# A graph network's last layer: eight outputs of each edge are summed over their 16 terms on VectorE before TensorE sums over the edges

## The chip, the cores and the metric

One core of a Trainium2 chip runs the whole program. The metric is device time in microseconds. A core has TensorE (PE, matrix products, with PEld for its weight loads), VectorE (DVE), ScalarE (ACT), GpSimd (POOL, which here issues indirect gathers) and SyncE (SP, which issues plain transfers). Each engine works through its own list in order, and they wait for one another through semaphores. TensorE writes into PSUM banks (`bank`); all else lies in SBUF, here in one large tile `f_arena`.

## The reference

Four graph layers run one after another over 8192 nodes of 32 values and 262144 edges sorted by destination. Each layer computes a message per edge, sums the messages at their destination, adds the result to the node and normalizes. The change is in the last layer. There an edge has its own weights, made from its 32 features by a small network:

```python
h = jax.nn.relu(edge_feat @ W1 + b1)
w = (h @ W2 + b2).reshape(e, 4, MUL, MUL)          # MUL = 8: 256 weights per edge
m0 = ALPHA * (einsum('ei,eio->eo', s_e * sh0, w_000)
              + C110 * einsum('eim,em,eio->eo', v_e, sh1, w_110))
m1 = ALPHA * (einsum('ei,em,eio->eom', s_e, sh1, w_011)
              + einsum('eim,eio->eom', v_e * sh0, w_101))
out0 = segment_sum(m0, dst); out1 = segment_sum(m1, dst)
```

Here s is the first 8 values of the source node, v the other 24 (8 vectors of 3), and sh the four values of the edge. So m0 has eight outputs per edge, each a sum of 8 + 8 = 16 products, and m1 has 24.

## The kernel before

Layers 0 to 2 run first and are untouched. Layer 3 goes over the edges in 512 quads. A quad `q` is four columns of 128 edges; eight quads make a batch `s` of 32 columns. Two quads, a pair, make one aggregation group `g` of 1024 edges.

For each quad the program does this:

- **Gather.** GpSimd fetches the source nodes' rows, one indirect transfer per column, 12 quads ahead (`fetch_rows`, `AHEAD = 12`, transfer at L380). The four gathers of quad q + 12 wait until quad q's weights are made (`quad[q]["w"]`).
- **Hidden layer.** Every second quad, `hidden` makes `h` for two quads: two matmuls (L836) and two ScalarE activations (L844).
- **Weights.** Four matmuls (L860) put the 4 x 256 weights into one of two PSUM buffers (`w_bank`). They wait for VectorE to be done with the quad before last.
- **Products on VectorE.** L897 multiplies weights with s for the w_011 part, and the result `pr` is reduced to 8 values one turn later (L889) and multiplied with sh into 24 columns (L884, two turns later). L900 makes the 128 products of m0 (8 outputs of 16 terms), and the three L904 make the 192 products of the w_101 part. L502 makes the one-hot matrix of destinations. The mark after L502 is `quad[q]["v"]`.
- **Sum over edges.** Four matmuls (L869) take the one-hot matrices as stationary operand and the products `p` as moving operand and add 1024 edges into a bank of 344 columns: 128 products of m0, 192 of the w_101 part and 24 finished. They stand three quads later in TensorE's list and wait for the mark `v` of the quad after next.
- **Evacuation.** After each second quad VectorE reduces the bank: 128 to 8 (L926), 192 to 24 (L927), and adds the 24 finished columns (L929) into the window `win`. Later `windows` and `normalize` put windows together into nodes.

Every eight quads `factors` (L778 to L789) prepares the next batch's `a0` and `vm` on VectorE.

The order on each engine is written out by hand in one loop `for q in range(NQ + 4)`. In a turn q, TensorE gets hidden(q + 2) on even turns, then the weights of q, then the sum over the edges of q - 3. VectorE gets, after `factors` where due, L884 of q - 2, L889 of q - 1, then waits for the weights of q and does L897, L900, L904 three times and L502, and on turns with q - 3 odd the evacuation. `p` has five buffers (`NP`), `pr` and `red` two.

Of the kernel before, what the change touches and what calls it, by code (L numbers as in the profile page):

```python
# [16 lines left out]
OP = mybir.AluOpType  # L17
AX = mybir.AxisListType
# [87 lines left out]
def in_order(ctx: ExitStack, tc, x, a, w0, w1, b1, w2, si, keep):  # L106
# [34 lines left out]
    with tc.tile_critical():  # L141
        raw_layers(tc, x, a, w0, w1, b1, w2, si, m, bad)
# [3 lines left out]
def raw_layers(tc, x, a, w0, w1, b1, w2, si, m, bad):  # L146
    nc = tc.nc
    PE, V, A, G, S = (Flow(tc, e, n) for e, n in ((nc.tensor, "pe"), (nc.vector, "dve"), (nc.scalar, "act"),
                                                  (nc.gpsimd, "pool"), (nc.sync, "sp")))
    bank, arena = m["bank"], m["arena"]  # L150
# [41 lines left out]
    cut = Carve()  # L192
# [10 lines left out]
    win = cut(GG, D)  # L203
    end0 = cut.at

    cut = Carve(8192)
    rg = cut(64, MS, 3)
    rgi = rg.rearrange("p a b c -> p (a b c)").bitcast(I32).rearrange("p (a b c) -> p a b c", b=MS, c=3)
    cut = Carve(8192)
    nxt = cut(TT, dt=I32)  # L210
    base = cut(GG, GT, dt=I32)
    cut = Carve()
# [177 lines left out]
    for j in range(NB // 4):  # L390
        for c in range(4):
# [4 lines left out]
            for h in range(2):  # L396
# [3 lines left out]
                for q in (2 * h, 2 * h + 1):  # L400
                    ins = PE.e.matmul(bank[:, 2 * b + q % 2, :], xT[q * D:(q + 1) * D, j, :],
                                      w0_s[q * D:(q + 1) * D, c * 512:(c + 1) * 512], start=True, stop=True)
# [3 lines left out]
                o, yp = ys[:, u, 2 * h:2 * h + 2, :], bank[:, 2 * b:2 * b + 2, :]  # L406
# [16 lines left out]
    def gathers(table, ix, s, t0=0, n=WT):  # L423

        if t0 == 0:
            state["n"] += 1
        k = (state["n"] - 1) % 4
        for t in range(t0, t0 + n):
            ld = g_ld[k][t // TP]
            if t % TP == 0:  # L430
                G.after(taken[k][t // TP])
                if len(under_way) >= LAG:
                    G.after(under_way[-LAG])
            indirect(xg[:, k, t, :], table[:, :], ix[:, s * WT + t:s * WT + t + 1]).then_inc(ld.sem, 16)
            ld.n += 16
            if t % TP == TP - 1:
                under_way.append(ld.mark())
        return k, under_way[-(WT // TP):]
# [58 lines left out]
    def ready(c):  # L497

        return min(GG, 4 * (LC * (c + 1) - 1) + 5)
# [93 lines left out]
    for g in range(GG):  # L593
        s, h, bk, c = g * GT // WT, g % NO, (g // per) % 2, g % per
        if g == FIRST // 2:
            V.after(slots(), x_in)
        if g * GT % WT == 0:
            k, landed = gathers(ytab, row, s)
# [5 lines left out]
        for t in range(GT):  # L604
            ins = PE.e.matmul(bank[:, bk, c * D:(c + 1) * D], oh[:, h, t, :], xg[:, k, g * GT % WT + t, :],  # L605
                              start=(t == 0), stop=(t == GT - 1))
# [17 lines left out]
    cut = Carve()  # L624
# [47 lines left out]
    for n, (l, c) in enumerate(seq):  # L672
# [8 lines left out]
        for s in range(64):  # L681
            if l == 1:
                q = s % 4
                ins = PE.e.matmul(bank[q * D:(q + 1) * D, b, 0:256].rearrange("p (u h j) -> p u h j", h=2, j=4),  # L684
                                  x_b[:, s, :], mv[:, s], start=(s < 4), stop=(s >= 60), tile_position=(0, q * D))
            else:
                ins = PE.e.matmul(bank[0:96, b, 0:512].rearrange("p (u h j) -> p u h j", h=2, j=4),  # L687
                                  x3[:, s, :], mv[:, s], start=(s == 0), stop=(s == 63))
# [13 lines left out]
    cut = Carve()  # L702
    xg = cut(4, WT, D)
    win = cut(GG, D)
# [13 lines left out]
    vs = cut(WT, 8, 3)  # L718
    a1 = cut(WT, 8)
    vm = cut(2, WT, 3, 8)  # L720
    MW = 344
    NP, NO = 5, 5
    p = cut(NP, 4, MW)
    pr = cut(2, 4, 64)
    red = cut(2, 4, 8)
    oh = cut(NO, 4, P)
    r1 = cut(24)
# [36 lines left out]
    def fetch_rows(q):  # L764

        if q < NQ:
            G.after(quad.get(q - AHEAD, {}).get("w"))
            rows[q // 8] = gathers(xtab, src, q // 8, q % 8 * 4, 4)
# [55 lines left out]
    def w_bank():  # L824
        k = nxt[0] % 2
        nxt[0] += 1
        return k, bank[:, 3 + 2 * k:5 + 2 * k, :].rearrange("p b (h c) -> p (b h) c", c=256)
# [24 lines left out]
    for q in range(NQ + 4):  # L852

        if q % 2 == 0 and q + 2 < NQ:
            hidden(q + 2)
        if q < NQ:
            k, wp = w_bank()
            PE.after(quad[q]["h"], w_free[k])
            for t in range(4):
                ins = PE.e.matmul(wp[:, t, :], hs[0:65, q % 4, t * P:(t + 1) * P], w2_s[0:65], start=True, stop=True)  # L860
            quad[q]["w"] = PE.mark(ins)
            quad[q]["k"] = k, wp
            fetch_rows(q + AHEAD)
        c = q - 3
        if 0 <= c < NQ:
            g = c // 2
            PE.after(quad[c + 2]["v"], agg_free[g % 2] if c % 2 == 0 else None)
            for t in range(4):
                ins = PE.e.matmul(bank[:, g % 2, 0:MW], oh[:, c % NO, t, :], p[:, c % NP, t, :],  # L869
                                  start=(c % 2 == 0 and t == 0), stop=(c % 2 == 1 and t == 3))  # L870
            quad[c]["a"] = PE.mark(ins)

        prev = (V.sem, V.n)
        if q % 8 == 6 and q // 8 + 1 < NS:
            s = q // 8 + 1
            factors(s)
        V.after(prev)
        if q < NQ:
            V.after(batch[q // 8]["f"])
        V.after(quad.get(q - NP, {}).get("a"))  # L880
        ins = None
        if 0 <= q - 2 < NQ:
            c = q - 2
            ins = V.e.tensor_tensor(p[:, c % NP, :, 320:344].rearrange("p t (o m) -> p t o m", m=3),  # L884
                                    red[:, c % 2, :, :, None].to_broadcast([P, 4, 8, 3]),
                                    sh[:, (c // 8) % 3, (c % 8) * 4:(c % 8) * 4 + 4, None, 1:4].to_broadcast([P, 4, 8, 3]),
                                    op=OP.mult)
        if 0 <= q - 1 < NQ:
            ins = V.e.tensor_reduce(red[:, (q - 1) % 2], pr[:, (q - 1) % 2].rearrange("p t (o i) -> p t o i", i=8),  # L889
                                    AX.X, OP.add)  # L890
        if q < NQ:
            k, wp = quad[q]["k"]
            s, u = q // 8, (q // 8) % 2
            qs = slice((q % 8) * 4, (q % 8) * 4 + 4)
            pq = p[:, q % NP]
            V.after(quad[q]["w"])
            V.e.tensor_tensor(pr[:, q % 2].rearrange("p t (o i) -> p t o i", i=8),  # L897
                              wp[:, :, 128:192].rearrange("p t (o i) -> p t o i", i=8),
                              xg[:, batch[s]["xg"], qs, None, 0:8].to_broadcast([P, 4, 8, 8]), op=OP.mult)
            V.e.tensor_tensor(pq[:, :, 0:128].rearrange("p t (o k) -> p t o k", k=16),  # L900
                              wp[:, :, 0:128].rearrange("p t (o k) -> p t o k", k=16),
                              a0[:, u, qs, None, :].to_broadcast([P, 4, 8, 16]), op=OP.mult)
            for mm in range(3):
                V.e.tensor_tensor(pq[:, :, 128 + 64 * mm:192 + 64 * mm].rearrange("p t (o i) -> p t o i", i=8),  # L904
                                  wp[:, :, 192:256].rearrange("p t (o i) -> p t o i", i=8),
                                  vm[:, u, qs, mm, None, :].to_broadcast([P, 4, 8, 8]), op=OP.mult)
            ins = one_hot(oh[:, q % NO], 4 * q, 4)
        if ins is not None:
            d = V.mark(ins)
            if q < NQ + 2:  # L910
                quad.setdefault(q, {})["v"] = d
            if q < NQ:
                w_free[k] = d
                if 4 * (q + 1) % TP == 0:
                    taken[batch[s]["xg"]][4 * (q % 8) // TP] = d
            if 0 <= q - 2 < NQ and (q - 2) % 8 == 7:
                s = (q - 2) // 8
                sh_free[s % 3] = d
                if s + 3 < NS:
                    fetch(s + 3)  # L920

        c = q - 3
        if 0 <= c < NQ and c % 2 == 1:
            g = c // 2
            V.after(quad[c]["a"])
            V.e.tensor_reduce(win[:, g, 0:8], bank[:, g % 2, 0:128].rearrange("p (o k) -> p o k", k=16), AX.X, OP.add)  # L926
            rm = V.mark(V.e.tensor_reduce(r1, bank[:, g % 2, 128:320].rearrange("p (mo i) -> p mo i", i=8), AX.X, OP.add))  # L927
            V.after(rm)
            gm = V.mark(V.e.tensor_tensor(win[:, g, 8:].rearrange("p (o m) -> p o m", m=3),  # L929
                                          bank[:, g % 2, 320:344].rearrange("p (o m) -> p o m", m=3),  # L930
                                          r1.rearrange("p (m o) -> p o m", o=8), op=OP.add))
            agg_free[g % 2] = gm
            while done < NB // LC and ready(done) <= g + 1:
                k, wp = w_bank()
                acc = bank[:, 3 + 2 * k, 0:LC * D]
                w_free[k] = normalize(3, done, acc, windows(done, acc, (w_free[k], gm)), z, x_a)
                done += 1
# [471 lines left out]
```

## Time and profile before

| | us |
|---|---|
| median of 3 runs | 7803.98 (7796.38 to 7807.71) |
| the profiled execution | 7682.45 |
| its span, first to last instruction | 7680.7 |
| busy in the span: TensorE | 5868.9 (76%) |
| VectorE | 3758.9 (49%) |
| ScalarE | 1653.0 (22%) |
| GpSimd | 4001.1 (52%) |
| layer 3, 4720 to 7560: TensorE, VectorE, GpSimd busy | 2540.9, 1956.5, 1873.0 of 2840 |

The profile is of one execution, and this one is shorter than the median of the timed runs by 121.5 us. A row of a group view gives the line, engine and operation, what it writes and reads, the shape, how many, the busy time and the mean of one in ns, and then the idle time of the engine just before these instructions with what ended most of it. An f32 matmul leaves two records, so four matmuls show as eight. The ends of matmuls are modelled, and a few records can be missing. In a timeline row stand the start, the duration, the engine, the line, the operation, and in brackets how long the engine had been idle before it and what is taken to have released it.

### The profile page before, as it was taken

The page shows a single profiled execution, that of the slowest core. Times are in us where ns is not written, and L with a number is a line of the kernel's source. Part 1 is how long each engine was busy: PE and PEld are TensorE (multiplying, and loading weights), DVE is VectorE, ACT ScalarE, POOL GpSimd, SP SyncE. Part 2 cuts the span into 40 slices and gives each one's busy share as a digit, 9 for nine tenths or more (in the row PEclk, how much of TensorE's full clock was granted, in tenths as well). Part 3 has the DMA queues.
Part 4 walks back from the last instruction along what each step waited for, and adds up shares of the span by engine and source line. Part 5 has one row for each costly group of instructions (what it writes and reads, how often), then busy time and mean ns, then how long its engine had stood idle before and what let it go on. Part 6 is the DMA issues. An engine that isn't in the chain of part 4 may idle for free.

```text
span 7680.7 us, 88486 instructions
## 1 busy us (share of the span) xinstructions
PE 5868.9 (76%) x36084; PEld 4261.6 (55%) x36084; DVE 3758.9 (49%) x6691; ACT 1653.0 (22%) x2828; POOL 4001.1 (52%) x4174
## 2 busy tenths in 40 slices
PE   5327777787877778786444776989898889888898
PEld 2116767776767667676222344555555555555555
DVE  3304444444444454544000004666666766676666
ACT  3123333333333333333000001111111111111111
POOL 3456656565656656561000006666666666666663
PEclk7556777777777777777777887999999899999999
DMA  8405655555555555567999981111111111111111
GB/s 285 144 10 125 144 141 143 142 145 140 143 142 145 148 134 151 136 149 217 432 432 429 403 336 26 24 24 24 24 24 27 24 24 24 24 24 24 24 24 19
DMA packets 290736, 999.46 MB, mean 130 GB/s; under 512 B 99022, under 2 KB 175887, under 8 KB 250639
## 3 DMA queue, kind: packets, MB, share of 16 engines
q1 hardware_dynamic: 155742, 916.89, 33.0%
q0 software_dynamic: 134144, 73.67, 9.4%
q8 instruction: 286, 4.69, 0.3%
q10 hardware_dynamic: 432, 3.15, 0.1%
q14 instruction: 132, 1.07, 0.1%
HBM read 521.39 MB, written 471.99 MB: 129 GB/s over the span
## 4 chain that ended last, share of the span: by engine, by line
PE 51%; DVE 15%; another core or an unknown queue 15%; DMA 10%; issue 6%; ACT 3%; SPq 0%; DVEq 0%; ACTq 0%
PE bank L869 16%; PE bank L568 15%; PE bank L860 9%; DMA f_arena<-famat 6%; PE bank L605 3%; PE bank L836 3%; DMA f_arena<-fcmat 3%; DVE f_arena L904 3%; DVE f_arena L502 2%; DVE f_arena L556 2%; PE bank L684 2%; PE bank L687 2%; DVE f_arena L900 2%; ACT f_arena L573 1%
## 5 line engine op out<-in xcount | busy, mean ns | idle before, releaser
L380 POOL DMA_INDIRECT f_arena<-fxtab,f_src x2048 | 1971.8, 963 | 2135.8 <-DVE f_arena L740 1111.0
L380 POOL DMA_INDIRECT f_arena<-fytab,f_row x2048 | 1962.0, 958 | 1338.6 <-issue 552.8
L568 PE MATMUL bank<-f_arena 64*128 64x128 f32 x16384 | 1846.0, 376 | 580.1 <-issue 416.2
L568 PEld LDWEIGHTS bank<-f_arena 64*128 64x128 f32 x16384 | 1619.5, 275 | 792.3 <-issue 572.6
L869 PE MATMUL bank<-f_arena 128*128 128x344 f32 x4096 | 1486.7, 511 | 288.6 <-DVE f_arena L502 284.2
L869 PEld LDWEIGHTS bank<-f_arena 128*128 128x128 f32 x4096 | 860.2, 214 | 764.2 <-DVE f_arena L502 348.7
L572 ACT ACTIVATE f_arena<-bank 128x512 bf16<-128x512 f32 x1024 | 612.3, 598 | 1886.7 <-remote 1163.8
L860 PE MATMUL bank<-f_arena 65*128 65x256 f32 x4096 | 1005.2, 388 | 0.0
L554 DVE TENSOR_TENSOR f_arena<-bank,f_arena 128x1024 f32<-128x1024 f32 x256 | 313.3, 1224 | 1363.4 <-remote 1281.6
L860 PEld LDWEIGHTS bank<-f_arena 65*128 65x128 f32 x4096 | 762.5, 191 | 357.3 <-issue 223.0
L844 ACT ACTIVATE f_arena<-bank,f_arena 64x512 f32<-64x512 f32 x512 | 351.1, 686 | 2530.8 <-PE bank L836 909.5
L502 DVE TENSOR_TENSOR f_arena<-bank,f_rel 128x512 f32<-128x512 f32 (+1 forms) x768 | 659.1, 859 | 246.1 <-ACT f_arena L534 233.6
L605 PE MATMUL bank<-f_arena 128*128 128x32 f32 x4096 | 545.3, 283 | 125.4 <-DMA f_arena<-fytab,f_row 69.0
L573 ACT ACTIVATE f_arena<-bank 128x512 f32<-128x512 f32 x1024 | 607.7, 593 | 0.0
L605 PEld LDWEIGHTS bank<-f_arena 128*128 128x128 f32 x4096 | 509.8, 199 | 155.2 <-issue 107.3
L556 DVE TENSOR_TENSOR f_arena<-bank,f_arena 128x2048 f32<-128x2048 f32 x256 | 586.6, 2291 | 8.8
L904 DVE TENSOR_TENSOR f_arena<-bank,f_arena 128x256 f32<-128x256 f32 x1536 | 551.3, 415 | 0.0
L684 PE MATMUL bank<-f_arena,f_x_b 128*32 128x256 f32 x4096 | 293.9, 458 | 335.5 <-DMA f_arena<-famat 335.5
L897 DVE TENSOR_TENSOR f_arena<-bank,f_arena 128x256 f32<-128x256 f32 x512 | 215.9, 422 | 660.8 <-PE bank L860 288.0
L684 PEld LDWEIGHTS bank<-f_arena,f_x_b 128*32 128x32 f32 x4096 | 145.5, 131 | 472.6 <-DMA f_arena<-famat 309.8
L900 DVE TENSOR_TENSOR f_arena<-bank,f_arena 128x512 f32<-128x512 f32 x512 | 348.8, 681 | 0.0
L687 PE MATMUL bank<-f_arena 128*96 128x512 bf16 x1024 | 248.7, 405 | 80.1 <-DMA f_arena<-fcmat 80.1
(127 smaller groups left out, 2628.1 us busy)
## 6 DMA issues: line engine op xcount, KB each, us to landing
famat<-f_arena SPq DMA_DIRECT2D x256, 1024.0 KB
fcmat<-f_arena SPq DMA_DIRECT2D x256, 512.0 KB
fytab<-f_arena SPq DMA_DIRECT2D x64, 1024.0 KB
f_arena<-fytab,f_row POOLq DMA_INDIRECT x2048
f_arena<-fxtab,f_src POOLq DMA_INDIRECT x2048
f_arena<-laid_ea SPq DMA_DIRECT2D x64, 512.0 KB
f_arena<-laid_ea SPq DMA_DIRECT2D x64, 64.0 KB
f_arena<-laid_xT ACTq DMA_DIRECT2D x1, 1024.0 KB, 8.0
```

The source lines that it names most:

```text
L380: return G.e.indirect_dma_start(out=dest, out_offset=None, in_=table, in_offset=bass.IndirectOffsetOnAxis(ap=ix, axis=0))
L502: return V.e.tensor_tensor(o, iota[:, None, :].to_broadcast([P, n, P]), rel[:, t:t + n, None].to_broadcast([P, n, P]), op=OP.is_equal)
L556: V.e.tensor_tensor(oh_l[:, b], iota[:, None, :].to_broadcast([P, 16, P]), meta_l[:, pp, k0:k0 + 16, None].to_broadcast([P, 16, P]), op=OP ...
L568: ins = PE.e.matmul(bank[:, bk + h, :].rearrange("p (c s j) -> p c s j", s=64, j=4)[:, :, :, j], oh_l[hs_, b, 4 * q + j, :], oh_k[hs_, b, ...
L572: A.e.activation(st_c[:, b, q], bank[:, bk:bk + 2, 0:256], AF.Copy)
L573: bank_free[units[0] % 2] = am = A.mark(A.e.activation(st_a[:, b, q], bank[:, bk:bk + 2, 256:512], AF.Copy))
L605: ins = PE.e.matmul(bank[:, bk, c * D:(c + 1) * D], oh[:, h, t, :], xg[:, k, g * GT % WT + t, :], start=(t == 0), stop=(t == GT - 1))
L684: ins = PE.e.matmul(bank[q * D:(q + 1) * D, b, 0:256].rearrange("p (u h j) -> p u h j", h=2, j=4), x_b[:, s, :], mv[:, s], start=(s < 4), ...
L860: ins = PE.e.matmul(wp[:, t, :], hs[0:65, q % 4, t * P:(t + 1) * P], w2_s[0:65], start=True, stop=True)
L869: ins = PE.e.matmul(bank[:, g % 2, 0:MW], oh[:, c % NO, t, :], p[:, c % NP, t, :], start=(c % 2 == 0 and t == 0), stop=(c % 2 == 1 and t = ...
L900: V.e.tensor_tensor(pq[:, :, 0:128].rearrange("p t (o k) -> p t o k", k=16), wp[:, :, 0:128].rearrange("p t (o k) -> p t o k", k=16), a0[: ...
L904: V.e.tensor_tensor(pq[:, :, 128 + 64 * mm:192 + 64 * mm].rearrange("p t (o i) -> p t o i", i=8), wp[:, :, 192:256].rearrange("p t (o i) - ...
```

## The change

The 128 products of m0 no longer go into `p`. They go into a buffer of their own, `p0`, with two places. One turn later VectorE adds up the 16 terms of each output and writes eight sums per edge into columns 0 to 7 of `p`. The other columns move down by 120, and the moving operand of the sum over edges has 224 columns instead of 344. After the sum, the first eight columns of the bank are already the outputs, so the reduction of 128 to 8 becomes a copy of 8. The number of matmuls, transfers and waits is the same, and VectorE gets one instruction more per quad (11682 rows of instructions in its list instead of 11170).

```diff
-    MW = 344
+    MW = 224
     NP, NO = 5, 5
     p = cut(NP, 4, MW)
+    p0 = cut(2, 4, 128)
...
-            ins = V.e.tensor_tensor(p[:, c % NP, :, 320:344].rearrange("p t (o m) -> p t o m", m=3),
+            ins = V.e.tensor_tensor(p[:, c % NP, :, 200:224].rearrange("p t (o m) -> p t o m", m=3),
...
         if 0 <= q - 1 < NQ:
+            V.e.tensor_reduce(p[:, (q - 1) % NP, :, 0:8], p0[:, (q - 1) % 2].rearrange("p t (o k) -> p t o k", k=16),
+                              AX.X, OP.add)
             ins = V.e.tensor_reduce(red[:, (q - 1) % 2], pr[:, (q - 1) % 2].rearrange("p t (o i) -> p t o i", i=8),
                                     AX.X, OP.add)
...
-            V.e.tensor_tensor(pq[:, :, 0:128].rearrange("p t (o k) -> p t o k", k=16),
+            V.e.tensor_tensor(p0[:, q % 2].rearrange("p t (o k) -> p t o k", k=16),
                               wp[:, :, 0:128].rearrange("p t (o k) -> p t o k", k=16),
                               a0[:, u, qs, None, :].to_broadcast([P, 4, 8, 16]), op=OP.mult)
             for mm in range(3):
-                V.e.tensor_tensor(pq[:, :, 128 + 64 * mm:192 + 64 * mm].rearrange("p t (o i) -> p t o i", i=8),
+                V.e.tensor_tensor(pq[:, :, 8 + 64 * mm:72 + 64 * mm].rearrange("p t (o i) -> p t o i", i=8),
...
-            V.e.tensor_reduce(win[:, g, 0:8], bank[:, g % 2, 0:128].rearrange("p (o k) -> p o k", k=16), AX.X, OP.add)
-            rm = V.mark(V.e.tensor_reduce(r1, bank[:, g % 2, 128:320].rearrange("p (mo i) -> p mo i", i=8), AX.X, OP.add))
+            V.e.tensor_copy(win[:, g, 0:8], bank[:, g % 2, 0:8])
+            rm = V.mark(V.e.tensor_reduce(r1, bank[:, g % 2, 8:200].rearrange("p (mo i) -> p mo i", i=8), AX.X, OP.add))
...
-                                          bank[:, g % 2, 320:344].rearrange("p (o m) -> p o m", m=3),
+                                          bank[:, g % 2, 200:224].rearrange("p (o m) -> p o m", m=3),
```

## Prediction

> **What bounds the kernel now.** I read the page's slices first. Layer 3 is slices 24 to 39, about 3.0 of 7.7 ms: TensorE nearly full, VectorE two thirds, GpSimd two thirds, clock 0.9.
>
> ```profile
> PE   5327777787877778786444776989898889888898
> DVE  3304444444444454544000004666666766676666
> POOL 3456656565656656561000006666666666666663
> PEclk7556777777777777777777887999999899999999
> ```
>
> Then the groups of layer 3's steady part, 4720 to 7560 us (243 pairs of quads, 11.67 us a pair; each f32 matmul has two records, so eight to a quad):
>
> ```profile
> L869 PE MATMUL bank<-f_arena 128*128 128x344 f32 x3892 | 1415.8, 512 | 280.7 <-DVE f_arena L502 276.2 <-issue 4.1
> L889 DVE TENSOR_REDUCE f_arena<-f_arena 128x32 f32<-128x256 f32 x486 | 200.4, 412 | 0.0
> L926 DVE TENSOR_REDUCE f_arena<-bank 128x8 f32<-128x128 f32 x243 | 68.8, 283 | 187.6 <-remote 66.0 <-PE bank L860 41.1 <-PE bank L869 40.9
> L787 DVE TENSOR_REDUCE f_arena<-f_arena 128x256 f32<-128x768 f32 x64 | 59.5, 929 | 0.0
> ```
>
> (L787 is from the same view over all of layer 3.) L869, which the change shortens, is the largest group, and only 281 us of idle stands before it. The chain of waits in this stretch is 41% L869, 21% L860, 8% L836. So TensorE looks like the bound. Two further views spoil that. First, who waited for whom:
>
> ```profile
> POOL f_arena L380 <- PE bank L860: 147.8, 70, 7.9
> POOL f_arena L380 <- PE bank L836: 117.4, 47, 2.6
> POOL f_arena L380 <- PE bank L869: 105.9, 65, 2.7
> POOL f_arena L380 <- remote: 54.2, 22, 2.6
> ```
>
> The gathers (L380) start 1.25 us apart (0.95 busy, 0.30 issue). Eight to a pair make 10.0 us; these 425 us of waits in 204 pieces (2.1 us each) add 1.75. That is the 11.7 us pair: GpSimd does nothing else. Second, the timeline around one such wait:
>
> ```profile
> 6003.73 1.07 PE L836 MATMUL bank<-f_arena 32*64 32x512 f32 x4
> 6004.74 1.99 PE L860 MATMUL bank<-f_arena 65*128 65x256 f32 x8
> 6006.57 2.48 PE L869 MATMUL bank<-f_arena 128*128 128x344 f32 x8
> 6008.89 1.89 PE L860 MATMUL bank<-f_arena 65*128 65x256 f32 x8
> 6010.11 1.40 ACT L844 ACTIVATE f_arena<-bank,f_arena 64x512 f32<-64x512 f32 x2 [15.75 <-PE bank L869]
> 6010.20 0.43 DVE L897 TENSOR_TENSOR f_arena<-bank,f_arena 128x256 f32<-128x256 f32 x1 [5.45 <-PE bank L869]
> 6010.44 0.95 POOL L380 DMA_INDIRECT f_arena<-fxtab,f_src  x1 [2.64 <-PE bank L869]
> 6012.87 4.14 PE L869 MATMUL bank<-f_arena 128*128 128x344 f32 x8 [2.09 <-DVE f_arena L502]
> ```
>
> L836 was over at 6004.8 and L860 at 6006.7, yet ScalarE, VectorE and GpSimd, which wait for them, all start at 6010.1 to 6010.4: TensorE's completions were seen 3 to 5 us late and together, after GpSimd had paused. After the last gather (7600) such lateness is gone: L836 then starts at 7616.32, 7625.62, 7634.92, a pair in 9.30 us with TensorE never idle. So the pair costs 9.3 us of matmul, 10.0 of gathers, and 11.7 in fact.
>
> **What the Trainium skill says.** "TensorE: Matmul & The Clock Gate", Back-to-back issue gap: a stream of matmuls goes by moving columns. The trace agrees: L869 to the next L860 is 2.33 us for 344 columns (0.29 a record), L860 to L869 1.73 for 256 (0.22). Same page, HAM oscillation: idle gaps throttle the clock. It agrees: after the 2.09 us gap above, L869 takes 4.14 us, not 2.48. "VectorE: DVE Perf Modes", The perf-mode tier table: a tensor_reduce has no faster mode than one element a cycle. It agrees: from 256 to 768 elements, 412 to 929 ns, 1.01 ns each. "SBUF — State Buffer", Who interferes with whom: an instruction with one SBUF input outside the two-port modes doesn't contend with GpSimd, so the new reduce shouldn't slow gathers. No run yet shows it.
>
> **The change, part by part.**
> (a) L869 goes from 344 to 224 columns: 2.33 x 224/344 = 1.51 us a quad, less 0.81 at full clock, 1.63 a pair. The weight load beside it (0.189 us a record in the stretch without gathers) equals the new 0.19, so it doesn't show; were loads alone to pace it, eight would still take 1.51. If all of it counted: 512 x 0.81 = 417 us, at the mean clock of 0.91 456.
> (b) One reduce more on VectorE per quad, 512 to 32 elements: 412 + 256 x 1.01 = 671 ns, or 0.59 from start to start, as the 512-element L900 and L502 (680 ns) show. 512 x 0.59 = 302 us of VectorE. It stands between L884 and L889, ahead of the wait for L860's result. Where VectorE waits there (the waits before L897 are 624 us in this stretch, 1.28 a quad) the wait hides it; where VectorE is late, L897 to L502, the next L869 and the release of the w bank all move 0.59 later.
> (c) L926 becomes a copy of 8 elements: nearest is L929, 24 elements, 183 ns; so -0.1 a pair, 26 us of VectorE, at the pair's end.
> (d) L900 writes another buffer, and the L904 and L884 columns move: nothing; same sizes and ports. The new reduce writes into p, which L869 reads only after a later VectorE mark that it waits for already. No DMA, wait or queue entry is added; fetch_rows, with its gathers, stands where it stood.
>
> Per pair: TensorE 9.30 - 1.63 = 7.67 at full clock; VectorE now 1956/243 = 8.05, then 8.05 + 1.18 - 0.10 = 9.1; gathers 10.0. Gathers become the longest of the three, and they were so before. What is left to win is thus the 425 us of GpSimd waits, not 456. These waits are ended by TensorE completions that come late for a reason which TensorE's speed does not remove.
>
> **The estimate.** GpSimd, 12 quads ahead, stops when the L860 result it waits for isn't announced. Two quads after a release that result stands 2 x 0.81 = 1.6 us earlier than now; the lateness spreads over some 0 to 6 us (5.45 above; longest 7.1 before L897). So 1.6/6, a quarter of the waits, could vanish. VectorE's extra 0.59 a quad and more throttled windows (TensorE is idle a third of the time) take back about half. 15% of 425 us is 64. The last stretch without gathers, six pairs, and the three closing L869 give 3 to 6 us, within this rounding. Profiled: 7682 - 64 = 7618. The median of the runs shown is 7804, 121 above the profiled execution; I carry the 64 over unscaled: 7740.
>
> **The rivals.**
> 1. The waits mostly go: TensorE has so much room that completions, late or not, reach GpSimd in time. Then the loop falls to 2048 x 1.25 = 2560 us plus a remainder. With 300 of the 425 gone: 7500; floor about 7380. For it: the chain is 70% TensorE. Against: the lateness above isn't matmul time.
> 2. Slower: VectorE takes over the loop. After a late L860 comes L897 to L502 (2.6 us), L869, L836, L860. One such round carries two quads and costs 2.6 + 2.33 + 1.0 + 1.83 = 7.8 us at full clock, so today's 11.67 holds some 3.9 of lateness and throttle. L869 takes 0.81 out of a round; the path gains 2 x 0.59 wherever the new reduce is not under a wait. It decides when over two thirds of the reduces are exposed and the throttle eats TensorE's gain: a clock of 0.75 instead of 0.91 turns 7.67 into 10.2, over the gathers. Price 0.3 us a pair, 75 us: 7880; with all 302 us exposed and nothing won, 8100.
> 3. It doesn't do what it says: p[.., 224] is not faster because each L869 waits for VectorE anyway (276 us of waits today). Then nothing changes: 7800.
>
> **How the numbers follow.** Main case 0.45, 7670 to 7800; rival 1 0.22; rival 2 0.25; rival 3 0.08. About 0.2% (16 us) is what a measurement of this kernel can tell from no change. Faster: most of the main case (0.38) and rival 1, 0.60; same 0.12; slower: rival 2 and a little of the main case, 0.28. Range 7520 to 7890: below it half of rival 1, above it the tail of rival 2.
>
> **What would show it.** Right: L869 mean near 340 ns and busy near 970 us; a new VectorE reduce of 512 to 32 at 0.67 us, its busy time up 270 us; gathers still 0.95 us, 1.25 apart; GpSimd's waits on TensorE still some 350 us; TensorE's busy share near 70% and its clock below 0.9. Rival 1: those waits under 150 us. Rival 2: L897 and L926 lose their idle time, and waits of L869 on L502 grow past 700 us. Wrong altogether: a gather whose mean changes, since everything here hangs on 1.25 us.

## The result: 0.36% slower, and the profile after

The changed kernel takes 7825.7 us (median of 19 runs, 7798.17 to 7851.4), the kernel before beside it on the same chip 7798.85 us (19 runs, 7772.61 to 7819.66). The ratio is 1.0036, with a 95% interval of 1.0025 to 1.0048. Chips differ in this study: the kernel before takes 7685 to 7799 us on most of them and 6476 to 6491 us on two, so every ratio below is taken against the kernel before on the same chip, unless another is named.

The profiled execution of the changed kernel took 7848.85 us (span 7847.0). Layer 3 begins at 4763 us in it and at 4671 us in the profile of before, although layers 0 to 2 are the same code; the two profiles were not taken side by side. Only what happens inside layer 3 is compared. I measure its loop in the traces from the start of the first hidden matmul to the end of the last sum over the edges: 2988.8 us before, 3063.5 us after. A second profile of the kernel before (e11 below) gives 2998.2, but it comes from a chip where the kernel before takes 7685 us, and the first one is as short. The changed kernel was profiled where the kernel before takes 7799 us. So the 75 us between the loops are not all the change's: side by side the two kernels are 27 us apart. Where the two profiles are compared below, I therefore name a pair from one chip too: the parts of the change run alone, e1 and e2.

The page's slices of the changed kernel (layer 3 is again slices 24 to 39):

```profile
PE   5327777777777777776455776878887878878777
DVE  3304444444444444445000005777777777777777
PEclk7556776677767777778777886888888888888888
```

In tenths of each slice, TensorE fell from 8 and 9 to 7 and 8, and VectorE rose from 6 and 7 to 7. So far this is what a shorter matmul and one more reduce must do. The line to read is the last: the clock that TensorE was granted fell from 9 to 8. The groups of layer 3 (the view by line and shape, 4660 to 7840 us):

```profile
L870 PE MATMUL bank<-f_arena 128*128 128x224 f32 x4096 | 1129.1, 429 | 559.4 <-DVE f_arena L502 470.8 <-issue 87.7
L861 PE MATMUL bank<-f_arena 65*128 65x256 f32 x4096 | 1105.3, 417 | 0.0
L890 DVE TENSOR_REDUCE f_arena<-f_arena 128x32 f32<-128x512 f32 x512 | 347.7, 679 | 0.0
L837 PE MATMUL bank<-f_arena 32*64 32x512 f32 x1024 | 321.5, 708 | 2.3 <-ACT f_arena L845 1.8 <-DVE f_arena L812 0.4
L929 DVE COPY f_arena<-bank 128x8 f32<-128x8 f32 x256 | 39.9, 156 | 241.0 <-PE bank L861 138.8 <-remote 43.7 <-PE bank L837 40.9
```

The sum over the edges (L870) went from 1486.7 us busy over the whole of layer 3 to 1129.1, 358 less. But two groups that the change doesn't touch grew: the weights (L861) from 1005.2 us, mean 388 ns, to 1105.3, mean 417; the hidden matmuls (L837) from 289.7, mean 643, to 321.5, mean 708. The same columns take longer because the clock is lower. Of 358 us won, 132 are gone at once, within TensorE.

The trace's own clock records say how. They show only full clock and half clock, in stretches that are whole multiples of 3.41 us. In the loop before there are 110 stretches at half clock, 505 us in all; in the changed kernel 127, 990 us. From one chip: 498 us with the reduce alone (e2), 1085 us with the narrower matmul alone (e1). They follow TensorE's idle time. In the changed kernel, 81 gaps of 3.41 us and more began at full clock, and in all 81 cases half clock came within the gap or 3.41 us after it. Of 43 gaps between 2 and 3.41 us 28 were followed so (42 of 43 before), and of 27 gaps under 1 us none (20 of 54 before).

Who waits for whom (4720 to 7700 us: total, number, longest):

```profile
PE bank L870 <- DVE f_arena L502: 450.3, 142, 5.9
POOL f_arena L380 <- PE bank L861: 343.9, 123, 19.4
POOL f_arena L380 <- remote: 88.7, 35, 2.9
POOL f_arena L380 <- PE bank L870: 86.4, 46, 2.9
POOL f_arena L380 <- PE bank L837: 12.0, 5, 2.8
```

The four rows of GpSimd, whose 425 us were all that could be won, now add up to 531 us (19 of them a single wait at the loop's start, which the stretch of before leaves out). TensorE, done sooner, waits for L502 on VectorE 471 us over the whole of layer 3 instead of 284. The timeline shows how one thing leads to the other:

```profile
6002.95 1.99 PE L861 MATMUL bank<-f_arena 65*128 65x256 f32 x8
6005.38 0.17 DVE L929 COPY f_arena<-bank 128x8 f32<-128x8 f32 x1 [5.20 <-PE bank L861]
6007.10 0.94 POOL L380 DMA_INDIRECT f_arena<-fxtab,f_src  x1 [2.72 <-remote]
6009.81 3.35 PE L870 MATMUL bank<-f_arena 128*128 128x224 f32 x8 [4.87 <-DVE f_arena L502]
6012.96 3.62 PE L861 MATMUL bank<-f_arena 65*128 65x256 f32 x8
6022.19 1.99 PE L861 MATMUL bank<-f_arena 65*128 65x256 f32 x8
6024.02 1.68 PE L870 MATMUL bank<-f_arena 128*128 128x224 f32 x8
6024.58 0.94 POOL L380 DMA_INDIRECT f_arena<-fxtab,f_src  x1 [2.42 <-PE bank L861]
6025.55 1.89 PE L861 MATMUL bank<-f_arena 65*128 65x256 f32 x8
```

The weights were made by 6004.9, and GpSimd goes on at 6007.1: the completion was seen late, as before the change. VectorE was held too, by an earlier one: L929 takes the sums of an L870 that had ended at 6002.0, and starts at 6005.4; it reaches the new weights at 6007.2. TensorE had nothing else to do and stood idle for 4.87 us. Then L870 takes 3.35 us for what takes 1.68 at 6024, and L861 3.62 instead of 1.99: half clock, which the clock records give from 6008.0 to 6021.6. So the weights that end at 6024.2 are not seen late but made late, and GpSimd waits another 2.42 us for them.

"Seen late" can be read closer than that. The trace records each step of the semaphore with which TensorE announces its work. In the stretch before that the prediction shows, L836, L860 and L869 end at 6004.81, 6006.73 and 6009.05, and the three steps are recorded at 6010.09, 6010.18 and 6010.27. So the waiting engines were not slow to look; the announcements themselves came late. Over the loop before, its last 100 us left out, 685 of 1234 came over 0.9 us after the end of their matmul, in the changed kernel 659 of 1232, in the same way (about a fifth of the steps are missing in these two traces, and where one is missing I took the next). ScalarE, which in the loop of layer 3 waits for L836 and little else, gives the same without them: 93 of its 256 starts in the loop before come over 0.9 us after the end of their matmul.

I sorted GpSimd's waits in the traces by this: how long had the L861 (L860) it waited for been over when the gather started? Over 0.9 us is "seen late", less is "made late". (The sum beyond the pitch counts starts more than 1.6 us apart; the two classes take those ahead of the first gather of a quad, the one that waits; clock from 5000 to 7000 us.)

| kernel | loop, us | clock | GpSimd beyond its 1.25 us pitch | seen late | made late |
|---|---|---|---|---|---|
| before | 2989 | 0.91 | 424 | 302 in 148 | 99 in 39 |
| changed | 3064 | 0.83 | 506 | 305 in 166 | 189 in 59 |
| e2, the reduce alone | 3016 | 0.91 | 448 | 311 in 165 | 120 in 31 |
| e1, the narrower matmul alone | 3033 | 0.82 | 480 | 274 in 143 | 191 in 49 |

The last two rows, of parts tried below, are from one chip. The waits for completions seen late hardly changed. Those for work made late almost doubled between the two profiles, and rose by 71 us from e2 to e1 on one chip. In the 8 us ahead of such a late L861 the mean clock was 0.60, against 0.85 ahead of all (before: 0.71 and 0.94).

### The profile page after: what moved, and what is told of

It reads as the page before. It is cut to its first block, busy times and chain, and to the rows that moved or that the text cites. A ratio compares the mean times of both kernels' runs of the same rounds, so it can differ in the third digit from the quotient of the medians.

```text
span 7847.0 us, 88998 instructions
## 1 busy us (share of the span) xinstructions
PE 5564.9 (71%) x36084; PEld 4419.2 (56%) x36084; DVE 4015.3 (51%) x7203; ACT 1646.0 (21%) x2828; POOL 3988.0 (51%) x4174
## 4 chain that ended last, share of the span: by engine, by line
PE 45%; DVE 17%; another core or an unknown queue 16%; DMA 10%; issue 6%; ACT 5%; SPq 0%; DVEq 0%; ACTq 0%
PE bank L568 15%; PE bank L870 10%; PE bank L861 8%; DMA f_arena<-famat 6%; PE bank L605 4%; DVE f_arena L907 3%; PE bank L837 3%; DMA f_arena<-fcmat 3%; DVE f_arena L502 2%; DVE f_arena L903 2%; ACT f_arena L573 2%; PE bank L684 2%; ACT f_arena L572 2%; PE bank L687 2%
## 5 line engine op out<-in xcount | busy, mean ns | idle before, releaser
L568 PE MATMUL bank<-f_arena 64*128 64x128 f32 x16384 | 1597.0, 365 | 447.8 <-issue 211.0
L568 PEld LDWEIGHTS bank<-f_arena 64*128 64x128 f32 x16384 | 1491.4, 272 | 557.3 <-issue 394.4
L870 PE MATMUL bank<-f_arena 128*128 128x224 f32 x4096 | 1129.1, 429 | 559.4 <-DVE f_arena L502 470.8
L870 PEld LDWEIGHTS bank<-f_arena 128*128 128x128 f32 x4096 | 932.9, 233 | 709.0 <-DVE f_arena L502 536.4
L861 PE MATMUL bank<-f_arena 65*128 65x256 f32 x4096 | 1105.3, 417 | 0.0
L861 PEld LDWEIGHTS bank<-f_arena 65*128 65x128 f32 x4096 | 834.5, 209 | 358.9 <-issue 240.0
L605 PE MATMUL bank<-f_arena 128*128 128x32 f32 x4096 | 691.0, 298 | 457.2 <-issue 374.1
L605 PEld LDWEIGHTS bank<-f_arena 128*128 128x128 f32 x4096 | 637.0, 225 | 490.1 <-issue 439.0
L502 DVE TENSOR_TENSOR f_arena<-bank,f_rel 128x512 f32<-128x512 f32 (+1 forms) x768 | 658.1, 858 | 247.4 <-ACT f_arena L534 234.8
L900 DVE TENSOR_TENSOR f_arena<-bank,f_arena 128x256 f32<-128x256 f32 x512 | 214.6, 419 | 425.0 <-PE bank L861 183.9
L890 DVE TENSOR_REDUCE f_arena<-f_arena 128x32 f32<-128x512 f32 x512 | 347.7, 679 | 0.0
```

The costliest lines, as they stand in the source:

```text
L502: return V.e.tensor_tensor(o, iota[:, None, :].to_broadcast([P, n, P]), rel[:, t:t + n, None].to_broadcast([P, n, P]), op=OP.is_equal)
L568: ins = PE.e.matmul(bank[:, bk + h, :].rearrange("p (c s j) -> p c s j", s=64, j=4)[:, :, :, j], oh_l[hs_, b, 4 * q + j, :], oh_k[hs_, b, ...
```

## Experiments: each part alone

**The TensorE part alone (e1).** 224 columns, the copy of 8, but no new reduce: `p[..., 0:8]` is zeroed once, so the eight outputs of m0 are left out.

```diff
-    MW = 344
+    MW = 224
+    p0 = cut(2, 4, 128)
+    for k in range(NP):
+        V.e.memset(p[:, k, :, 0:8], 0.0)
...
(the other lines as in the change, without the new tensor_reduce)
```

> The 224 columns on TensorE without the new reduce on VectorE: the first eight columns of p are zeros written once, so the eight m0 outputs are left out. Theory A (the loop of layer 3 is paced by the gathers and by TensorE's completions, which are announced late while GpSimd gathers): TensorE's saving is worth little, 7740 to 7800 us beside 7799 before. Theory B (TensorE's saving is real and the reduce on VectorE eats it up): the saving shows here, 7400 to 7550 us.

Measured: 7748.4 us against 7711.18, ratio 1.0043 (1.0028 to 1.0057). So the loss doesn't need the reduce. Both theories had the kernel no slower than before. With 417 us of full-clock matmul taken away and nothing put in, the kernel is slower, with the lower clock of the whole change (0.82) and as much waiting for work made late (191 us).

**The VectorE part alone (e2).** The kernel before with the extra reduce into a scratch tile.

```diff
+    p0s = cut(4, 8)
...
+            V.e.tensor_reduce(p0s, p[:, (q - 1) % NP, :, 0:128].rearrange("p t (o k) -> p t o k", k=16), AX.X, OP.add)
```

> The kernel before with 344 columns, and the reduce of 512 to 32 added on VectorE at the same place, into a scratch that nothing reads. Theory A: the reduce mostly hides in VectorE's waits, 7800 to 7840 us. Theory B: the reduce costs what the change gave back, 7950 to 8100 us.

Measured: 7744.44 us, ratio 1.0033 (1.0017 to 1.0048), at a clock of 0.91. The reduce costs 33 us of its 302. The parts don't add up: 0.43% and 0.33% alone, 0.36% together.

## Experiments: without the gathers

**e3 and e4: the kernel before, and the changed one, with the gathers of layer 3 beyond the first 32 quads left out** (the products then use rows fetched earlier).

```diff
-        if q < NQ:
+        if 32 <= q < NQ:
+            rows[q // 8] = rows[q // 8 % 4]
+        elif q < NQ:
```

> The kernel before, but in layer 3 only the first four batches of rows are gathered and later batches use them again (wrong rows for 60 of 64 batches). Theory A: without gathers completions come on time and a pair of quads takes the 9.3 us of TensorE's work; loop of layer 3 about 2390 us instead of 2990, total about 7200. If the late completions have nothing to do with the gathers: 11 to 11.7 us a pair, 7650 to 7800.

> The changed kernel with the same cut of the gathers. Theory A: now VectorE's 9.1 us a pair paces, loop about 2340 us, total about 7150, some 50 faster than the kernel before without gathers. Theory B (the VectorE round is the bound): slower than the kernel before without gathers, 7250 or more.

Measured: e3 7241.43 us (ratio 0.9385), loop 2514 us, 9.82 a pair where 9.3 were expected, clock 0.99; only 4 of ScalarE's 256 starts are late, all before the last gather. So the late announcements go with the gathers.

e4 has two paces. Three of its four executions took 7403 to 7429 us, at a clock of 0.756 to 0.758 over the whole program; the fourth took 7211.74 us at 0.778. Beside e3 three are 162 to 187 us slower, and one is 30 us faster. So e4 doesn't settle whether the changed kernel must lose without gathers; it shows that the same program can run some 200 us apart, with the clock. The profile is of a long one (7403 us): loop 2690, 10.51 a pair, clock 0.84. In it half clock comes once in each batch: 66 stretches, of which 63 last 13.65 us.

**e10: the TensorE part alone, without gathers** (m0 left out as in e1, gathers as in e3).

> The PE part alone (eight m0 outputs left out, no new reduce) without the gathers after the fourth batch. No engine has more to do than in the kernel before without gathers (7241 us), TensorE has 1.6 us a pair less. Theory C: clock under 0.9 and the time not below 7241, up to 7400. Theory D (the VectorE reduce made e4 slow): 7000 to 7150, VectorE's 8.05 us a pair being the bound.

Measured: 7080.46 us, ratio 0.9213 (0.9195 to 0.923), loop 2396, 9.36 a pair. Here the narrower matmul does pay, though at a clock of 0.92: the loop is 118 us shorter than e3's. That is what Theory D expected, and against Theory C: without gathers the lower clock alone doesn't make the kernel lose. (e3 and e4 ran on one chip, e9 and e10 on another, so I compare loops, or ratios, and not times.) From e10 to e4's profile the loop grows by 294 us, about the whole 302 of the new reduce, with the clock going from 0.92 to 0.84.

**e9: the changed kernel without gathers, with TensorE kept busy.** Four matmuls of 192 columns into unused columns of the bank, on odd quads, ahead of the wait for `v`; gathers left out as in e4.

```diff
-            PE.after(quad[c + 2]["v"], agg_free[g % 2] if c % 2 == 0 else None)
+            PE.after(agg_free[g % 2] if c % 2 == 0 else None)
+            for t in range(4 if c % 2 else 0):
+                PE.e.matmul(bank[:, g % 2, 256:448], oh[:, c % NO, t, :], p[:, c % NP, t, 8:200], start=False, stop=False)
+            PE.after(quad[c + 2]["v"])
```

> The changed kernel without the gathers after the fourth batch (as e4), and with the filling matmuls of e5 on every second quad. e4 took 7403 to 7429 us in three runs and 7212 in one, at a clock of 0.76 and 0.78 over the run. Theory C (short of work, TensorE falls to half clock and then is the bound itself): with TensorE kept busy the clock in layer 3 is 0.97 or more and every run takes 7200 to 7260 us, 2% less than e4 although TensorE does more. If the clock is only a symptom: 7400 to 7500.

Measured: 7225.54 us (four executions, 7221.51 to 7233.14), ratio 0.9405 (0.9386 to 0.9423), loop 2530. More work, and the loop is 160 us shorter than in e4's profile; against e4's one quick execution, at 0.9352 of the kernel before, nothing is won. The view of one stretch, 5000 to 7000 us (busy time of TensorE, its weight loads, VectorE, ScalarE, GpSimd, each with its number of instructions, then clock, DMA share, GB/s), first e4, then e9:

```profile
5000.00:7000.00 2000.00, 1793.58 (x6981) 1371.29 (x6980) 1732.35 (x4350) 265.94 (x394) 0.00 (x0) 0.84 0.05 15
```

```profile
5000.00:7000.00 2000.00, 1908.67 (x9049) 1560.10 (x9050) 1842.28 (x4626) 284.71 (x422) 0.00 (x0) 0.98 0.05 16
```

The clock went from 0.84 to 0.98 and VectorE got through 6% more instructions (4626 for 4350). Half clock fell from 874 us in 66 stretches to 119 in 11. So filled, the program kept to the quick pace in four of four executions, unfilled in one of four. What the three long executions lose without gathers goes with the throttle (the lower clock that TensorE is granted): VectorE, busy for 1842 of 2000 us, has little room once TensorE answers at half clock.

**e5, e6, e7: the same filling with the gathers in place**, in the changed kernel, in its TensorE part (m0 left out), and with 96 columns in the kernel before.

> The changed kernel, with four matmuls of 192 columns on every second quad, put before TensorE's wait for VectorE's mark, into unused columns of the bank. They do nothing but keep TensorE busy (1.3 us a pair at full clock). Theory C (the change loses because TensorE, with less to do, runs at half clock for part of the time): the clock in layer 3 goes from 0.82 back to 0.9, L870's neighbour L861 from 417 ns back to under 400, and the time falls below the changed kernel's, at or under the kernel before: 0.0 to 2% faster than before. Theory D (the added VectorE reduce makes the loss): the filling only adds work, 0.4 to 2% slower than before.

> The same filling in the kernel with the PE part alone (eight m0 outputs left out, no new reduce). Theory C: clock 0.9 or more, and the shorter L869 now pays: 1 to 4% faster than before, against 0.43% slower without the filling. Theory A (the late completions alone pace the loop): no gain, within 0.5% of before.

> The kernel before with a filling of 96 columns on every second quad. Theory C in a strong form (any idle TensorE window costs more than the work that would fill it): clock above 0.91, 0.3 to 1.5% faster. Otherwise, since TensorE was already 89% busy: 0 to 2% slower.

Measured: 1.0088 (1.0069 to 1.0106), 1.0075 (1.0058 to 1.0092), 1.0051 (1.0034 to 1.0068); clocks 0.88, 0.86, 0.95; GpSimd's waits 526, 528 and 485 us. Theory C, that the loss is the clock's, forecast a gain for e5 and e6, and both lost more than without the filling (1.0036 and 1.0043, on other chips). The filling brought only part of the clock back, and TensorE was still idle for 352 us of the loop in e5 and 329 in e6; that it also stood ahead of real work when a completion came is my reading and was not tested. With gathers in place, then, the clock as the cause of the loss stands on the timeline and the counts above, and the one experiment that raised it speaks against the clock alone.

## Experiments: what holds the completions back

**e8: plain transfers instead of gathers.** SyncE loads rows of the same table, the same bytes, so other rows than the edges name.

```diff
-            G.after(quad.get(q - AHEAD, {}).get("w"))
-            rows[q // 8] = gathers(xtab, src, q // 8, q % 8 * 4, 4)
+            S.after(quad.get(q - AHEAD, {}).get("w"), taken[k][t0 // TP])
+            S.e.dma_start(xg[:, k, t0:t0 + 4, :], xtab[v:v + 512, :].rearrange("(t p) f -> p t f", p=P)).then_inc(ld.sem, 16)
...
```

> The kernel before, with the rows of layer 3 fetched by one plain transfer per quad from SyncE's queue in the place of four gathers by GpSimd (rows in order, so not the right ones; the same bytes). If the late completions come from GpSimd's gathers: loop of layer 3 about 2510 us as without gathers, total some 6% under before. If they come from the transfers as such: loop near 2990 us, total within 1.5% of before.

Measured: 7215.75 us, ratio 0.927 (0.9251 to 0.9288), loop 2501 us, clock 0.99. The bytes are there and the lateness isn't: no start of ScalarE is late, and every announcement of TensorE is recorded within 0.03 us. On this chip it comes with the gathers as GpSimd issues them. (e8 also has one transfer for four gathers, so it doesn't say which trait of them does it.)

**e12: one announcement less per pair.** The sum over the edges is announced on odd quads only (`p` and `oh` get six buffers).

```diff
-            quad[c]["a"] = PE.mark(ins)
+            if c % 2:
+                quad[c]["a"] = quad[c - 1]["a"] = PE.mark(ins)
```

> The kernel before with one announcement less per pair: L869 of an even quad is no longer marked, its buffers are freed by the mark of the odd quad after it, and p and oh have six places instead of five. If TensorE's late announcements pass one at a time while GpSimd gathers (theory A), four instead of five per pair make GpSimd's waits shorter: 0.5 to 2% faster than before. If their number doesn't matter: within 0.3%.

**e11: the kernel before again**, one execution on the same chip.

> The kernel before, unchanged, for a second profile: loop of layer 3 between 2980 and 3020 us, GpSimd's waits beyond its 1.25 us pitch 420 to 450 us, clock 0.90 to 0.92, if the first profile is typical of it.

Measured: e12 7685.07 us, ratio 1.0000 (0.9994 to 1.0007), 299 us seen late; e11 7690.02 us, 309 us. My guess that completions queue up behind one another, and that fewer of them would come sooner, is not borne out for one fewer of five.

**e13, e14, e15: GpSimd paused.** Before each eight gathers GpSimd waits for the eight before, not for those before them; in the kernel before, the changed one, and the TensorE part (m0 left out).

```diff
+    LAG = 1
```

> The kernel before, but in layer 3 GpSimd waits before each eight gathers until the eight before them have landed (LAG = 1 in place of 2), some 0.8 us of pause per pair. If a regular short pause lets TensorE's completions through, the late waits (300 us of GpSimd's stalls) shrink by more than the pause costs: 1 to 3% faster. If only a pause of 2 us and more does, the pause is mostly hidden in stalls that are there anyway: within 1%, either way.

> The changed kernel with the same pause. If the change loses because held completions leave TensorE idle and then at half clock: with fewer held completions the gap to the kernel before closes or turns, ratio to e13 0.98 to 1.00. If it loses by VectorE's reduce: ratio to e13 1.005 or more.

> The PE part alone (eight m0 outputs left out) with the same pause. It was 0.43% slower with the gathers and 2.2% faster without them. With fewer held completions it should lie between: 0.97 to 1.00 of e13. If the pause changes nothing about them: 1.004 of e13.

These ran on a chip where the kernel before takes 6490.98 us. Measured: 7070.04, 7013.73 and 6983.14 us, so the changed kernel is at 0.9920 of e13 and the TensorE part at 0.9877. The pause itself costs 8.9%, where at most 1% was expected, since GpSimd's waits for landing rows join the loop (334 us from 3900 to 6400 us; e13's loop is 3197 us). In that loop, with room on every engine, the narrower matmul pays, although the clock in the loop falls from 0.88 (e13) to 0.81: a lower clock is not a loss by itself. What the pause does to late completions these runs can't say, for on this chip there are none: not one start of ScalarE in the three loops is late. Why the unpaused kernel is so much quicker there had to be read in the kernels as they are.

## Experiments: a chip without late completions

**e16, e17, e18: the kernel before, the changed one and the TensorE part (m0 left out), unaltered**, on another chip of the quicker kind.

> The kernel before, unchanged, with a profile. Theory: its layer 3 is 2560 us of gathers and some 425 to 440 us of GpSimd waits. On a chip where it takes 7690 to 7790 the loop of layer 3 is 2990 to 3000 us and the clock there 0.91. If it takes near 6490, as on the chip of the paused kernels, then the completions are hardly held back there: loop near 2600 us, GpSimd waits beyond the 1.25 pitch under 100 us. If the waits are still 400 us there, the gain of that chip lies in layers 0 to 2 alone.

> The changed kernel, unchanged. Theory (held completions turn the time won on TensorE into idle time and a lower clock): 1.002 to 1.006 of before where before takes about 7700. Where before takes near 6490 and completions are not held, the loop is paced by gathers alone, and the change makes no difference in the loop: 0.998 to 1.002. Rival (the clock falls with the idle time whether completions are held or not): 1.003 or more on either chip.

> 224 columns without the new reduce (the eight outputs of m0 stay zero, so that part of the computation is left out). Same theory: 1.003 to 1.006 where before takes about 7700, 0.997 to 1.001 where it takes near 6490. Rival: 1.003 or more on either.

| kernel | us | ratio (interval) | loop | a pair | GpSimd beyond pitch | seen late | made late |
|---|---|---|---|---|---|---|---|
| before | 6475.84 | 1.0 (0.9992 to 1.0009) | 2610.6 | 10.20 | 16 | 4 | 1 |
| changed | 6556.21 | 1.0121 (1.0105 to 1.0138) | 2693.6 | 10.52 | 101 | 2 | 75 |
| TensorE part | 6461.02 | 0.9976 (0.9968 to 0.9985) | 2597.4 | 10.15 | 14 | 5 | 2 |

On this chip the gathers hold nothing back: all 1231 announcements of TensorE in the loop of e16 are recorded within 0.03 us, 302 us seen late become 4, and the kernel before runs at the gathers' own pace (2048 x 1.25 = 2560 us). Layers 0 to 2 end at 3839 us instead of 4671. I had written that then the change makes no difference. It costs 1.2%, as the rival in e17's expectation had it, and the TensorE part gains 0.24%, so here the loss needs the reduce. The stretch from 4200 to 6200 us, the kernel before and then the changed one (columns as above):

```profile
4200.00:6200.00 2000.00, 1918.65 (x7220) 1252.79 (x7219) 1593.93 (x4103) 276.18 (x410) 1514.84 (x1587) 0.98 0.14 28
```

```profile
4200.00:6200.00 2000.00, 1785.75 (x6980) 1365.29 (x6979) 1732.95 (x4356) 265.90 (x394) 1468.11 (x1534) 0.84 0.13 27
```

The second is e4's row again, with gathers in it: VectorE 1733, clock 0.84, 10.5 us a pair. It has e4's half-clock stretches too, one for nearly every batch: 63, of which 60 last 13.65 us, 860 us in all, against 26 and 137 us in e16. Here all four executions are alike (6553 to 6557 us). The changed kernel has a cycle of its own of 10.5 us, longer than the gathers' 10.0, in this profile with gathers and in e4's without. The timeline shows where it comes from (the changed kernel, once in eight quads):

```profile
5019.66 0.21 DVE L779 TENSOR_SCALAR f_arena<-f_arena 128x128 f32<-128x128 f32 x1
5023.52 0.30 DVE L790 TENSOR_SCALAR f_arena<-f_arena 128x256 f32<-128x256 f32 x1
5027.51 3.36 PE L870 MATMUL bank<-f_arena 128*128 128x224 f32 x8 [4.04 <-DVE f_arena L502]
5030.79 1.97 PE L837 MATMUL bank<-f_arena 32*64 32x512 f32 x4
5032.69 3.78 PE L861 MATMUL bank<-f_arena 65*128 65x256 f32 x8
5036.52 0.43 DVE L900 TENSOR_TENSOR f_arena<-bank,f_arena 128x256 f32<-128x256 f32 x1 [3.56 <-PE bank L861]
5036.75 0.94 POOL L380 DMA_INDIRECT f_arena<-fxtab,f_src  x1 [0.86 <-PE bank L861]
```

`factors` (L779 to L790) puts 4 us of VectorE between two quads. TensorE, now quicker than VectorE, has no backlog and stands idle for 4.04 us; it then runs L870, L837 and L861 at half clock, and VectorE waits 3.56 us for L861 in its turn, while GpSimd is 0.86 late. In the kernel before (e16), at the same place, L869 is at half clock (4.27 us instead of 2.48), and L836 is already at full clock again:

```profile
5030.49 4.27 PE L869 MATMUL bank<-f_arena 128*128 128x344 f32 x8 [2.58 <-DVE f_arena L502]
5034.69 1.07 PE L836 MATMUL bank<-f_arena 32*64 32x512 f32 x4
```

Over the loop (3900 to 6400 us), the changed kernel:

```profile
PE bank L870 <- DVE f_arena L502: 269.9, 67, 16.5
DVE f_arena L900 <- PE bank L861: 244.5, 118, 3.6
POOL f_arena L380 <- PE bank L861: 108.7, 113, 7.1
```

and the kernel before:

```profile
DVE f_arena L897 <- PE bank L860: 374.4, 186, 4.1
PE bank L869 <- DVE f_arena L502: 104.4, 62, 13.0
```

TensorE's wait for L502, which comes about once in a batch, went from 104 to 270 us. The TensorE part has it too (324.6 us in 70, clock 0.88), yet loses nothing: without the reduce VectorE makes up for the lost time before the next batch. So on this chip it takes both, the idle time and a VectorE with little to spare. That the clock is what stretches the cycle here is argued from e9, where the filled loop without gathers takes 9.88 us a pair; no filled kernel ran on this chip.

## Why the prediction was wrong

**Right.** What bounds the loop: GpSimd's gathers and its waits, not TensorE. The gather kept its 0.96 us and its pitch of 1.25, with the new reduce beside it; the waits for completions seen late stayed near 300 us, for a reason that TensorE's speed does not remove (of the 425 us the prediction put down to them, 99 were for work made late); TensorE's busy share fell to 71% and its clock below 0.9. The prices: the reduce 679 ns against 671, the copy 156 against 183, VectorE's busy time up 256 us against 270.

**Part (a), the mean of L869.** 340 ns and 970 us busy were said, 429 ns and 1129 us came out. At full clock the 1.51 us a quad is right: in the stretch above an L870 starts at 6024.02 and the L861 behind it at 6025.55, 1.53 us later, and a record of L870 that lies wholly at full clock has a mean of 356 ns. Those at half clock have 593: the clock makes most of the difference.

**The step that failed: "a quarter of the waits, could vanish ... more throttled windows take back about half".** I let the L860 result stand 1.6 us earlier two quads after each release, and valued the throttle at a share of that gain. But while a completion is held back, TensorE has its next work only after the release; what it saves is then spent idle, and idle time is followed by half clock. Half clock in the loop went from 505 to 990 us (498 to 1085 on one chip, e2 and e1), and made-late waits rose by 90 us between the profiles (71 on one chip) where 106 us of waits were to vanish. The give-back was no half but more than the whole: -64 us were forecast, +27 us came. What the runs show is this rise of half clock and of work made late, without the reduce too (e1); that the one causes the other is read from the timeline, and the filled kernels e5 and e6 did not confirm it.

**The sum per pair.** TensorE 7.67, VectorE 9.1, gathers 10.0 were each right for an engine alone at full clock, and gave the gathers the last word. The loop through TensorE and VectorE takes 10.51 us a pair (e4) at the clock that it brings about itself, and 9.88 when TensorE is kept busy (e9). That was rival 2's thought, with the clock 0.84 and not 0.75; it came true where completions come in time (e17), on a chip that the forecast was not about. On the chips where they come late, its signs stayed half out: L900 and L929 still had 425 and 241 us of idle time, and TensorE's waits for L502 came to 471 us, not 700. There the narrower matmul loses by itself (e1), which neither the main case nor a rival had.

**What stays open.** Why gathers hold TensorE's announcements back on some chips and not on others. The profiled executions of the kernel before are 1210 us apart (7682 against 6472). Layers 0 to 2 have the same lateness, 642 of 1205 announcements between 600 and 3500 us against 17 of 1214, but that all of the 1210 us come from it is not shown. The bytes moved (e8) and one announcement in five (e12) are not the cause on the chips that do. Not tried: a way to take the half clock away while the gathers run, filled kernels on the chip without late completions, and the reduce on another engine.

## What to carry to other kernels

When engines wait for one another in a ring, time taken from one of them is worth nothing unless it shortens the ring. On TensorE it may be worth less than nothing (0.43% slower in e1), since here idle time was followed by half clock for the matmuls that remained. So cost a change to a ring as a round trip at the clock that its gaps will leave, not as three engines side by side, and look where one engine inserts a block once per batch (here `factors`): that is where a lost backlog shows. Before trusting a small gain, ask whether the late events in the trace are work made late or completions seen late; shorter work cures only the first.

## What the runs showed of the hardware

- TensorE's granted clock was full or half and nothing between, in stretches of whole multiples of 3.41 us, in every loop read here. Idle gaps of 2.09 us and 2.58 us were followed by a matmul group at about half clock, and ones of 4.04 and 4.87 us by three groups. "TensorE: Matmul & The Clock Gate" in the Trainium skill, HAM oscillation, names gaps above about 3.4 us; here shorter ones did it too: 42 of 43 gaps between 2 and 3.41 us in the loop before, 28 of 43 in the changed kernel.
- A loop without gathers that fell to half clock once in each batch (2690 us, clock 0.84) took 2530 us when TensorE was given matmuls whose result nobody reads (clock 0.98; e4, e9).
- With indirect gathers running, over half of TensorE's announcements in the loop before came more than 0.9 us late on one chip (685 of 1234), and none of 1231 on another. The gathers that waited for them started 3.7 us after the matmul's end in the median of 148 cases (5.2 of 166 in the changed kernel). The pitch of the gathers was 1.25 us on both chips.
